# A graph attention layer on one core: longer DMA runs, four neighbouring nodes a partition, and Q in float32

## The chip, the cores and the metric

The kernel runs on one core of a Trainium2 chip. Five engines work side by side: TensorE (PE, with its weight loads shown apart as PEld), VectorE (DVE), ScalarE (ACT), GpSimd (POOL) and SyncE (SP), which issues most of the plain DMAs. The metric is the device time of one execution in microseconds; less is better. A profiled execution has a span, from its first to its last instruction, and a time that is a little longer.

## What is computed

The graph has 12500 nodes with 128 features and 212500 edges, sorted by destination. With 8 heads of 16 features:

```
Q, K, V = x @ WQ, x @ WK, x @ WV            # per node, then split into 8 heads
Eh      = edge_attr @ WE                    # per edge
score   = K[src] * Q[dst] / sqrt(16) * Eh
score   = exp(clip(score.sum(-1), -5, 5))   # one number per edge and head
wV, Z   = segment_sum(V[src] * score, dst), segment_sum(score, dst)
h       = x + wV / (Z + 1e-6)
y       = x + batchnorm(h) * gamma + beta   # statistics over all nodes
out     = layernorm(y)                      # per node
```

Everything is float32.

## The kernel before, in words

Edges come in tiles of 128, 1661 tiles in all. A *unit* is up to 4 tiles whose destinations lie in a window of 64 nodes; a *group* is two units, so 8 tiles, and there are NG = 208 groups. The two halves of a group sit on the upper and lower 64 partitions wherever nodes are on partitions.

**Table stage.** `table_rows` (L634) multiplies node features by WK and WV (L641: the features, `hx`, are the stationary operand, 128 columns of nodes at a time) and copies the products out with ACT and DVE in turn (L249, L250). Each call does four blocks of 128 nodes. A DMA on SP (L649) writes them to the table `kvd` in DRAM: node `c * 128 + p` comes from partition `p`, so one run is the 1 KB of one node. Meanwhile GpSimd gathers the source features of the first 8 groups straight from `x` (64 gathers); for these groups K and V are computed per edge (`project`, `project_main`).

**Gathers.** For all other groups GpSimd issues one indirect DMA per tile (L202): 128 rows of 1 KB from `kvd` into a slot. There are eight slots and one more that comes free later; a slot is free again when the `message` of its group is done (L580). `pace` and `issue` (L208 to L218) put the gathers in their places among the other engines' steps.

**Main loop** (L759). Iteration g runs, for several groups at once, the steps of a hand-written order. SP loads edge attributes for group g+4 (`load`, L433, three buffers of 4 KB a partition) and the *places*: for each edge of a unit, its destination's number inside the window. The places were turned by PE and written to `relT` in DRAM by `place` (L313); `load_rel` (L338) reads one group's, `load_quad` (L327) four groups' at once, spread over 64 partitions a half, four runs of 1 KB in each. On PE: `q_mm` (L483) makes Q of the window's nodes, `gather_sum` (L596, L595) adds the messages up by a one-hot matrix, `eh_mm` (L510) makes Eh, `turn_back` (L543) transposes, `qe_mm` (L525) spreads Q to the edges: the stationary operand is Q, the moving one a one-hot matrix of the places (`turned_onehot`, L473, bf16). Q is float32 and is split into three bf16 parts whose products are added: `q_out` (L487), `q_hi` (L491) and `q_mid` (L498) on ACT, `q_rest` (L495) and `q_lo` (L501) on DVE; so `qe_mm` has six matmuls a group, three for each half. On DVE further: `products` (L558), `scores` (L565), `both` (L535), `attn` (L612), `message` (L580), `onehot` (L463 to L466).

**Last stage** (L896). When the last group is added in, the batch norm's statistics are closed and 25 tiles of up to 512 nodes are centred, scaled and written. PE subtracts the mean over the features and turns nodes onto partitions in one matmul, with the nodes' features as the stationary operand: `part_of_x` (L740) and L941 for the nine tiles of `AHEAD`, L952 for the others, in which GpSimd or DVE first form the sum. Seven of the L740 tiles come before this stage begins. ACT squares (L967, L972), DVE scales (L984), and L986 writes 512 nodes with one DMA, 512 B a run. The last tile has 212 nodes. `load_x` (L414) brings the features back for this stage, in four DMAs of 512 columns a slot.

The lines of the changed functions and of their callers follow.

Of the kernel before, what the change touches and what calls it, by code (L numbers as in the profile page):

```python
# [21 lines left out]
G = 8  # L22
# [38 lines left out]
def gnn_kernel(  # L61
# [42 lines left out]
    kvd = dram.tile([N, 2 * P], F32, name="kvd")  # L104
    relT = dram.tile([T, P], BF16, name="relT")

# [81 lines left out]
    def slot(i):  # L188
        return rows.tile([P, 2 * G * P], F32, name=f"slot{i}")
# [123 lines left out]
    def place(r):  # L313
        nc.vector.tensor_copy(vw(rel, r), vw(rel_i, r))
        nc.vector.tensor_tensor(vw(rel, r), vw(rel, r), bc(base_f, r), op=OP.subtract)
        end = ustarts[r[0]] + (r[1] - r[0]) * r[2]
        for t in range(ustarts[r[0]], end, P):
            n = min(P, end - t)
            ps = spare_ps
            nc.tensor.transpose(ps[:n], rel[:, t:t + n], ident)  # L320
            row = wp.tile([P, P], BF16, name="relrow", bufs=2)
            nc.vector.tensor_copy(row[:n], ps[:n])  # L322
            nc.scalar.dma_start(relT[t:t + n, :], row[:n])

    RB = {}

    def load_quad(q):  # L327
        t = late[0].tile([P, RQ, U * P], BF16, name="rbq", bufs=2)
        for h in (0, 1):
            at = ustarts[2 * RQ * q + h] * P  # L330
            nc.sync.dma_start(t[h * WN:(h + 1) * WN], bass.AP(
                tensor=relT.tensor, offset=relT.offset + at, ap=[[0, WN], [G * P, RQ], [1, U * P]]))
        for k in range(RQ):
            RB[RQ * q + k] = t[:, k, :]

    quads = range(-(-2 * LATE // RQ), sizes.count(G) // RQ)

    def load_rel(g):  # L338
        if g // RQ in quads:
            return  # L340
        RB[g] = wp.tile([P, U * P], BF16, name="rb", bufs=3)
        for h in (0, 1):
            t, n = ustarts[2 * g + h], usizes[2 * g + h]
            nc.sync.dma_start(RB[g][h * WN:(h + 1) * WN, :n * P],
                              bass.AP(tensor=relT.tensor, offset=relT.offset + t * P, ap=[[0, WN], [1, n * P]]))

# [67 lines left out]
    def load_x():  # L414
        t = slot(free.pop(0))
        for k in range(4):
            if todo:
                i = todo.pop(0)
                XR[i] = t[:, k * B4:(k + 1) * B4]
                nc.sync.dma_start(XR[i][:, :width(i)], xT[:, i * B4:i * B4 + width(i)])  # L420

    EA, OH, OT, Q3, XW, BASE, MSG, QE, OS, AT, AGG, WT, PW = ({} for _ in range(13))

# [18 lines left out]
    def q_window(g):  # L442
        if g not in BASE:
            n = 2 if g % 2 == 0 and g + 1 < NG else 1
            _, at = nc.values_load_multi_w_load_instructions(
                base_i[0:1, 2 * g:2 * (g + n)], engines=(ET.Activation,), min_val=0, max_val=N,
                skip_runtime_bounds_check_because="node ids")
            for k in range(n):
                BASE[g + k] = at[2 * k:2 * k + 2]
        XW[g] = wp.tile([P, P], F32, name="xw", bufs=8)  # L450
        for h in (0, 1):
            nc.scalar.activation(XW[g][:, h * WN:(h + 1) * WN], hx[:, ds(BASE[g][h], WN)], AF.Copy)  # L452
# [16 lines left out]
    def turned_onehot(g):  # L469

        OT[g] = wp.tile([P, U * P], BF16, name="ot", bufs=2)
        if usizes[2 * g] == usizes[2 * g + 1] == U:
            nc.vector.tensor_scalar(OT[g], RB[g], wiota, None, op0=OP.is_equal)  # L473
# [5 lines left out]
    PQ, QS, QR = {}, {}, {}  # L479

# [4 lines left out]
    def q_out(g):  # L485
        QS[g] = wp.tile([P, P], F32, name="qs", bufs=2)
        nc.scalar.activation(QS[g], PQ[g], AF.Copy, scale=0.25)  # L487

    def q_hi(g):
        Q3[g] = wp.tile([P, 3, P], BF16, name="q3", bufs=2)  # L490
        nc.scalar.activation(Q3[g][:, 0, :], QS[g], AF.Copy)  # L491

    def q_rest(g):
        QR[g] = QS[g]
        nc.vector.tensor_sub(QR[g], QS[g], Q3[g][:, 0, :])  # L495

    def q_mid(g):
        nc.scalar.activation(Q3[g][:, 1, :], QR[g], AF.Copy)  # L498

    def q_lo(g):  # L500
        nc.vector.tensor_sub(Q3[g][:, 2, :], QR[g], Q3[g][:, 1, :])  # L501

# [17 lines left out]
    def qe_mm(g):  # L520
        QE[g] = [psp.tile([P, U * P], F32, name="ps_q", bufs=2)[:, :(b - a) * P] for a, b in halves(g)]
        for k in range(3):
            for h, (a, b) in enumerate(halves(g)):
                r = slice(h * WN, (h + 1) * WN)
                nc.tensor.matmul(QE[g][h], Q3[g][r, k, :], OT[g][r, :(b - a) * P], start=(k == 0), stop=(k == 2))  # L525

# [105 lines left out]
    NB = -(-N // P)  # L632

    def table_rows(b):  # L634
        t = table_tile(b // 4)
        for q in range(b, min(b + 4, NB), 2):
            ps = wide()
            m = min(2, NB - q)
            for i in range(m):
                n = min(P, N - (q + i) * P)  # L640
                nc.tensor.matmul(ps[:n, i, :], hx[:, (q + i) * P:(q + i) * P + n], w_kv, start=True, stop=True)  # L641
            fl = min(m, N // P - q)
# [4 lines left out]
        full = min(4, N // P - b)  # L647
        if full > 0:
            nc.sync.dma_start(kvd[b * P:(b + full) * P, :].rearrange("(c p) d -> p c d", p=P), t[:, :full, :])  # L649
# [11 lines left out]
    def both_halves(g):  # L661
# [3 lines left out]

    steps = [[(locate,)], [(place, runs[0])], [], [(q_mm, 0), (q_out, 0), (q_hi, 0)],
             [(q_rest, 0), (q_mid, 0), (load_rel, 0)], [(q_lo, 0), (load, 0)],
             [(q_mm, 1), (q_out, 1), (q_hi, 1), (load_rel, 1)],
             [(q_rest, 1), (q_mid, 1)], [(q_lo, 1), (load_rel, 2)], [(load, 1)], [(turned_onehot, 0)],
             [(turned_onehot, 1)]]  # L670
# [24 lines left out]
    table[0] = True  # L695
    load_kv()
    ehqe(0)
    q_mm(2)
    q_out(2)
    q_hi(2)  # L700
    both_halves(0)
    q_rest(2)
    q_mid(2)
    turn_back(0)
    ehqe(1)
    within(load, 2)
    turned_onehot(2)
    load_rel(3)
    q_window(3)
    q_window(4)  # L710
    q_mm(3)
    q_out(3)
    load_rel(4)
    load(3)
    onehot(0)
# [18 lines left out]
    def blocks(i):  # L734
        n = width(i)
        return [(k, min(P, n - k * P)) for k in range(-(-n // P))]

    def part_of_x(i, ps):
        for k, m in blocks(i):
            nc.tensor.matmul(ps[:m, k, :], XR[i][:, k * P:k * P + m], cent, start=(k == 0), stop=False)  # L740

# [17 lines left out]
    for g in range(NG - 2):  # L759
        within(load, g + 4)  # L760
        within(load_rel, g + 5)
        if (g + 6) % RQ == 0 and (g + 6) // RQ in quads:
            load_quad((g + 6) // RQ)
        within(q_hi, g + 3)
        within(products, g)
        within(q_lo, g + 2)
        within(denom, g - 2)
        within(scores, g)
        within(clip_exp, g)
        within(recip, g - 2)  # L770
        within(turned_onehot, g + 3)
        within(both_halves, g + 1)
# [4 lines left out]
        within(add_x, g - 3)  # L777
        within(q_mm, g + 4)
        if g < LATE + 4:
# [10 lines left out]
        within(x_out, g - 3)  # L790
        within(q_out, g + 4)
        within(sums_out, g - 1)
# [3 lines left out]
        within(eh_out, g + 2)  # L796
        within(q_window, g + 5)
        within(turn_back, g + 1)
        within(qe_mm, g + 2)
        within(attn, g - 2)  # L800
        within(q_rest, g + 3)
        within(q_mid, g + 3)
        within(message, g)
# [92 lines left out]
    def last_stage(fin, bank, PX):  # L896
# [35 lines left out]
        def centred(i):  # L932
# [16 lines left out]
            if not full:  # L949
                whole = i in on_vector  # L950
                for k, m in blocks(i):
                    nc.tensor.matmul(ps[:m, k, :], Y[i][:, k * P:k * P + m], cent, start=not whole,  # L952
                                     stop=(k == 3 or not whole))
# [22 lines left out]
        def scaled(p):  # L976
# [3 lines left out]
            for h, i in enumerate(p):  # L980
                bl = blocks(i)
                c, fb = i * B4, sum(m == P for _, m in bl)
                if fb:
                    nc.vector.tensor_tensor(o[:, h, :fb, :], PY[i][:, :fb, :],  # L984
                                            v[:, h, :fb, :].to_broadcast([P, fb, P]), op=OP.mult)
                    (nc.scalar if i == NY - 2 else nc.sync).dma_start(  # L986
                        out[c:c + fb * P, :].rearrange("(c p) d -> p c d", p=P), o[:, h, :fb, :])
                for k, m in bl[fb:]:
# [161 lines left out]
```

## Time and profile before

| | |
|---|---|
| median of 3 runs | 2141.86 us (2141.61 to 2143.22) |
| the profiled execution, its time | 2143.53 us |
| its span | 2141.1 us |
| mean granted PE clock | 0.917 of full speed |
| instructions | 31269 |
| DMA | 386.41 MB, mean 180 GB/s |
| DMA packets | 172648, 88727 of them under 2 KB |

In a row of groups stand the line, the engine, the operation, what it writes and reads, the shapes and the count; then the busy time in us and the mean of one in ns; then the idle time of the engine before them, and what ended it. In a row of the timeline stand the start and the duration in us, the engine, the line, the operation and, in brackets, the idle time before it. In a row of the windows stand the length, then the busy time and count of PE, PEld, DVE, ACT and POOL, the granted clock, the DMA engines' busy share and GB/s. In a row of DMA issues stand the count, the KB of each and the median us from issue to landing. PE's records of one float32 matmul are two, each with a weight load of its own.

### The profile page before, as it was taken

To read this page: it belongs to the slowest core of one execution; us is meant where nothing else is said; L and a number is where in the kernel's file an instruction comes from. 1 tells how busy PE (TensorE), PEld (TensorE's weight loads), DVE (VectorE), ACT (ScalarE), POOL (GpSimd) and SP (SyncE) were. 2 spreads that over 40 slices of the span, in tenths; PEclk is the share of its full clock that TensorE was granted. 3 is DMA by queue.
4 is the path that set the end of the run, shared out by engine and by line. 5 is a ranking of instruction groups with operands and counts; after the bars stand their busy time and mean duration, and the time that the engine had idled before them with its cause. 6 is when DMAs were issued, how large, how long until landed. Compare 5 with 4: busy or idle time off the path is not lost. (4 is left out here: it accounts for less than half of the span.)

```text
span 2141.1 us, 31269 instructions
## 1 busy us (share of the span) xinstructions
PE 1710.7 (80%) x9414; PEld 1100.9 (51%) x9414; DVE 1590.1 (74%) x3555; ACT 670.6 (31%) x2688; POOL 1606.6 (75%) x1697
## 2 busy tenths in 40 slices
PE   8899998777868778877778778777878877778777
PEld 7576565444545445544445445545545545544456
DVE  4679998777777777777677777677777777777786
ACT  3454343223223223222223223223223222223225
POOL 7777777777777777777777777777777777777775
PEclk9999999998998998899898998898898898898899
DMA  9957666565565565565565565565565565565574
GB/s 306 308 177 201 188 198 183 165 182 166 165 183 158 171 183 163 167 183 165 165 183 158 172 183 163 167 184 160 169 184 159 170 184 161 167 184 164 170 235 125
DMA packets 172648, 386.41 MB, mean 180 GB/s; under 512 B 35950, under 2 KB 88727, under 8 KB 172471
## 3 DMA queue, kind: packets, MB, share of 16 engines
q0 software_dynamic: 78704, 213.62, 34.6%
q1 hardware_dynamic: 90404, 169.36, 25.9%
q8 instruction: 78, 1.28, 0.3%
q10 hardware_dynamic: 3363, 1.34, 0.2%
q14 instruction: 99, 0.81, 0.1%
HBM read 364.56 MB, written 19.63 MB: 179 GB/s over the span
## 5 line engine op out<-in xcount | busy, mean ns | idle before, releaser
L202 POOL DMA_INDIRECT slot<-kvd,srcs x1597 | 1517.8, 950 | 486.4 <-issue 409.4
L558 DVE TENSOR_TENSOR slot<-slot,ps_t 128x512 f32<-128x512 f32 x410 | 276.7, 682 | 453.2 <-DMA slot<-kvd,srcs 412.3
L543 PE MATMUL ps_t<-ident,wt 128*128 128x128 f32 x1661 | 283.9, 313 | 385.9 <-DVE wt L535 384.1
L596 PE MATMUL ps_a<-msg,oh 128*128 128x136 f32 (+1 forms) x3322 | 524.4, 297 | 2.1 <-DVE msg L580 2.1
L543 PEld LDWEIGHTS ps_t<-ident,wt 128*128 128x128 f32 x1661 | 211.7, 159 | 562.3 <-issue 501.2
L596 PEld LDWEIGHTS ps_a<-msg,oh 128*128 128x128 f32 (+1 forms) x3322 | 425.2, 171 | 81.5 <-issue 53.8
L575 ACT ACTIVATE ps_m<-s 128x64 f32<-128x64 f32 (+1 forms) x209 | 47.5, 227 | 1125.4 <-DVE s L574 1060.9
L510 PE MATMUL ps_e<-ea,w_e 128*128 128x512 f32 x832 | 390.6, 591 | 0.7 <-ACT wt L517 0.7
L535 DVE TENSOR_TENSOR wt<-wt,ps_q 128x512 f32<-128x512 f32 x416 | 264.4, 675 | 2.6 <-PE ps_q L525 2.6
L580 DVE TENSOR_TENSOR msg<-slot,ps_m 128x1024 f32<-128x1024 f32 (+2 forms) x209 | 248.0, 1188 | 0.4 <-ACT ps_m L575 0.3
L565 DVE TENSOR_REDUCE s<-slot 128x64 f32<-128x1024 f32 (+1 forms) x208 | 248.1, 1194 | 0.1
L517 ACT ACTIVATE wt<-ps_e 128x512 f32<-128x512 f32 x416 | 233.8, 620 | 13.3 <-PE ps_e L510 13.2
L525 PE MATMUL ps_q<-ot,q 64*128 64x512 bf16 x1248 | 213.3, 457 | 0.0
L510 PEld LDWEIGHTS ps_e<-ea,w_e 128*128 128x128 f32 x832 | 143.0, 190 | 100.7 <-issue 98.5
L463 DVE TENSOR_TENSOR oh<-ps_m,rel_i 128x512 f32<-128x512 f32 x208 | 141.4, 680 | 0.0
L491 ACT ACTIVATE q<-qs 128x128 bf16<-128x128 f32 x208 | 64.3, 309 | 217.3 <-PE ps_q L525 186.6
L621 PEld LDWEIGHTS ps_a<-ident,at 128*128 128x128 f32 x408 | 71.7, 221 | 111.7 <-issue 56.0
L621 PE MATMUL ps_a<-ident,at 128*128 128x128 f32 x408 | 115.4, 370 | 2.5 <-DVE relrow L322 2.3
L626 ACT ACTIVATE hx<-ps_a 128x64 f32 x408 | 87.9, 215 | 33.9 <-PE ps_a L596 27.2
L452 ACT ACTIVATE xw<-hx 128x64 f32 x416 | 88.2, 280 | 11.1 <-DMA hx<-xT 6.5
L525 PEld LDWEIGHTS <-q 64*128 64x128 bf16 x1248 | 48.9, 103 | 80.9 <-issue 64.4
L622 PE MATMUL ps_a<-xw,ident 128*128 128x128 f32 x408 | 89.7, 306 | 0.0
(175 smaller groups left out, 1618.9 us busy)
## 6 DMA issues: line engine op xcount, KB each, us to landing
ea<-eaT SPq DMA_DIRECT2D x207, 512.0 KB, 3.8
slot<-kvd,srcs POOLq DMA_INDIRECT x1597
rbq<-relT SPq DMA_DIRECT2D x94, 256.0 KB, 6.6
kvd<-slot SPq DMA_DIRECT2D x12, 512.0 KB, 7.1
kvd<-t SPq DMA_DIRECT2D x12, 512.0 KB, 6.8
slot<-xT SPq DMA_DIRECT2D x24, 256.0 KB, 5.2
out<-o SPq DMA_DIRECT2D x23, 256.0 KB, 3.2
hx<-xT SPq DMA_DIRECT2D x11, 512.0 KB, 7.7
```

The lines of the kernel that those rows point to most:

```text
L202: return nc.gpsimd.indirect_dma_start(out=out, out_offset=None, in_=table, in_offset=bass.IndirectOffsetOnAxis(ap=srcs[:, e:e + 1], axis=0))
L463: nc.vector.tensor_tensor(one, iota_ps[:, None, :].to_broadcast([P, n, P]), r[:, :n, None].to_broadcast([P, n, P]), op=OP.is_equal)
L510: nc.tensor.matmul(eh, w_e, EA[g][:, a:b, :].rearrange("p a b -> p (a b)"), start=True, stop=True)
L517: nc.scalar.activation(t[:, :(b - a) * P], EH[g][h], AF.Copy)
L525: nc.tensor.matmul(QE[g][h], Q3[g][r, k, :], OT[g][r, :(b - a) * P], start=(k == 0), stop=(k == 2))
L535: nc.vector.tensor_tensor(t, t, QE[g][h], op=OP.mult)
L543: nc.tensor.transpose(ps[:, j, :], WT[g][h][:, j * P:(j + 1) * P], ident)
L558: step = nc.vector.tensor_tensor(kv, kv, PW[g][i][:, :b - a, :], op=OP.mult)
L565: step = nc.vector.tensor_reduce(SS[g][:, a:b, :], KV[g](a, b, 0).rearrange("p t (h d) -> p t h d", d=DH), axis=AX.X, op=OP.add)
L580: step = nc.vector.tensor_tensor(MSG[g][:, a:b, :P].rearrange("p t (h d) -> p t h d", d=DH), KV[g](a, b, P).rearrange("p t (h d) -> p t h ...
L596: nc.tensor.matmul(AGG[g][WN if j >= n else 0:], OH[g][j], MSG[g][:, j, :], start=(j == 0), stop=(j == n - 1))
L621: nc.tensor.matmul(ps, AT[g], ident, start=True, stop=False)
```

## The change

- `load` fetches the attributes of two groups in one DMA: 8 KB a run for 4 KB, two buffers of two groups for three of one.
- `place` orders the turned places so that all first units stand together in `relT` and all second units after them (a DVE copy ahead of the transpose, and two DMAs for one); the places past the last full group go to a second tensor, `rel_end`. Four groups' places of a half are then one run of 4 KB for four of 1 KB.
- `table_rows` takes every fourth column of 512 nodes as the stationary operand, so that a partition holds four neighbouring nodes and the write to `kvd` has runs of 4 KB for 1 KB. The last stage does the same in L740, L941 and L952, and its writes have runs of 2 KB for 512 B. Tiles that aren't full stay as they were.
- `load_x` fetches a slot's features in one DMA.
- Q stays in one float32 tile, the turned one-hot is float32 too, and `qe_mm` has two matmuls a group. `q_hi`, `q_rest`, `q_mid` and `q_lo` are gone.
- Some steps run for a group one or two later in the order: `load_rel` g+3 for g+5, `q_mm` and `q_out` g+2 for g+4, `turned_onehot` g+2 for g+3, `q_window` g+3 for g+5; buffers of `rb` 2 for 3, `xw` 6 for 8, `qs` 1 for 2.

```diff
     def load_quad(q):
         for h in (0, 1):
-            at = ustarts[2 * RQ * q + h] * P
-            nc.sync.dma_start(t[h * WN:(h + 1) * WN], bass.AP(
-                tensor=relT.tensor, offset=relT.offset + at, ap=[[0, WN], [G * P, RQ], [1, U * P]]))
+            nc.sync.dma_start(t[h * WN:(h + 1) * WN].rearrange("p a b -> p (a b)"), places(h, RQ * q, RQ))
...
-    def load(g):
-        n = nt(g)
-        EA[g] = wp.tile([P, G, P], F32, name="ea", bufs=3)
-        nc.sync.dma_start(EA[g][:, :n, :].rearrange("p a b -> p (a b)"),
-                          eaT[:, starts[g] * P:(starts[g] + n) * P])
+    def load(i):
+        gs = range(2 * i, min(2 * i + 2, NG))
...
+        t, n = wp.tile([P, 2, G, P], F32, name="ea", bufs=2), sum(nt(g) for g in gs)
...
+        nc.sync.dma_start(t.rearrange("p c a b -> p (c a b)")[:, :n * P],
+                          eaT[:, starts[2 * i] * P:(starts[2 * i] + n) * P])
...
-        OT[g] = wp.tile([P, U * P], BF16, name="ot", bufs=2)
+        OT[g] = wp.tile([P, U * P], F32, name="ot", bufs=2)
...
-        for k in range(3):
-            for h, (a, b) in enumerate(halves(g)):
-                r = slice(h * WN, (h + 1) * WN)
-                nc.tensor.matmul(QE[g][h], Q3[g][r, k, :], OT[g][r, :(b - a) * P], start=(k == 0), stop=(k == 2))
+        for h, (a, b) in enumerate(halves(g)):
+            r = slice(h * WN, (h + 1) * WN)
+            nc.tensor.matmul(QE[g][h], QS[g][r], OT[g][r, :(b - a) * P], start=True, stop=True)
...
+    def every_fourth(a, k):
+        return a.rearrange("p (n c) -> p n c", c=4)[:, :, k]
...
-                nc.tensor.matmul(ps[:n, i, :], hx[:, (q + i) * P:(q + i) * P + n], w_kv, start=True, stop=True)
+                at = every_fourth(hx[:, b * P:(b + 4) * P], q + i - b) if b + 4 <= N // P else \
+                    hx[:, (q + i) * P:(q + i) * P + n]
+                nc.tensor.matmul(ps[:n, i, :], at, w_kv, start=True, stop=True)
...
+            nc.sync.dma_start(kvd[b * P:(b + 4) * P, :].rearrange("(p c) d -> p c d", c=4), t)
...
+    def nodes(a, i, k, m):
+        return every_fourth(a[:, :B4], k) if width(i) == B4 else a[:, k * P:k * P + m]
...
-            nc.tensor.matmul(ps[:m, k, :], XR[i][:, k * P:k * P + m], cent, start=(k == 0), stop=False)
+            nc.tensor.matmul(ps[:m, k, :], nodes(XR[i], i, k, m), cent, start=(k == 0), stop=False)
...
-        within(load, g + 4)
-        within(load_rel, g + 5)
+        if g % 2 == 0:
+            load(g // 2 + 2)
+        within(load_rel, g + 3)
...
-        within(q_hi, g + 3)
         within(products, g)
-        within(q_lo, g + 2)
...
-        within(turned_onehot, g + 3)
+        within(turned_onehot, g + 2)
...
-        within(q_mm, g + 4)
+        within(q_mm, g + 2)
...
-                    nc.tensor.matmul(ps[:m, k, :], hx[:, c + k * P:c + k * P + m], scaled_cent, start=False,
+                    nc.tensor.matmul(ps[:m, k, :], nodes(hx[:, c:c + width(i)], i, k, m), scaled_cent, start=False,
                                      stop=False)
...
-                    nc.tensor.matmul(ps[:m, k, :], Y[i][:, k * P:k * P + m], cent, start=not whole,
+                    nc.tensor.matmul(ps[:m, k, :], nodes(Y[i], i, k, m), cent, start=not whole,
```

More of the change, by code (lines that the diff above doesn't have):

```diff
@@ L663, in both_halves @@
         both(g, 1)
[L666 to L669, printed above, removed]
+    steps = [[(locate,)], [(place, runs[0])], [], [(q_mm, 0), (q_out, 0)],
+             [(load_rel, 0)], [(load, 0)], [(load_rel, 1)], [], [], [], [(turned_onehot, 0)],
              [(turned_onehot, 1)]]
@@ L696, in gnn_kernel @@
     load_kv()
+    load(1)
+    load_rel(2)
     ehqe(0)
-    q_mm(2)
-    q_out(2)
-    q_hi(2)
+    q_mm(1)
+    q_out(1)
     both_halves(0)
-    q_rest(2)
-    q_mid(2)
     turn_back(0)
     ehqe(1)
[L706 to L714, printed above, removed]
     onehot(0)
@@ L790, in gnn_kernel @@
         within(x_out, g - 3)
-        within(q_out, g + 4)
+        within(q_out, g + 2)
         within(sums_out, g - 1)
@@ L796, in gnn_kernel @@
         within(eh_out, g + 2)
-        within(q_window, g + 5)
+        within(q_window, g + 3)
         within(turn_back, g + 1)
```

75 lines of the change are left out of this document (43 added, 32 removed).

## The prediction

> **What bounds the kernel now.** I read the engine totals first, then the groups of GpSimd (POOL), then its timeline at both ends.
>
> ```profile
> PE 1710.7 (80%) x9414; PEld 1100.9 (51%) x9414; DVE 1590.1 (74%) x3555; ACT 670.6 (31%) x2688; POOL 1606.6 (75%) x1697
> ...
> L202 POOL DMA_INDIRECT slot<-kvd,srcs x1597 | 1517.8, 950 | 486.4 <-issue 409.4
> ```
> ```profile
> L202 POOL DMA_INDIRECT slot<-x,srcs x64 | 60.8, 951 | 21.1 <-issue 14.6 <-DMA slot<-x,srcs 2.7 <-DMA srcs<-src 1.9
> ```
> ```profile
> 3.04 1.15 POOL L202 DMA_INDIRECT slot<-x,srcs  x1 [1.87 <-DMA srcs<-src]
> ...
> 2085.13 0.95 POOL L202 DMA_INDIRECT slot<-kvd,srcs  x1 [0.30 <-issue]
> 2086.38 0.95 POOL L202 DMA_INDIRECT slot<-kvd,srcs  x1 [0.30 <-issue]
> ```
>
> By busy shares PE looks like the bound; it isn't. The 1597 gathers take 950 ns each with 486.4 / 1597 = 0.305 us before each, and the last rows show 0.30 as the plain step from one gather to the next. From 3.04 to 2087.33 us there are 1661 gathers, 1.255 us apiece on average, back to back: none waits for a slot, for the table or for a semaphore long enough to show. So the time is three parts: 3.0 us until the first gather, 2084.3 us of gathers, 53.8 us after the last one. An edit counts only where it (a) shortens or lengthens a gather, (b) makes GpSimd wait, or (c) touches the last 53.8 us. Almost all of this change, the DMA runs above all, is none of these.
>
> The last part has a bound of its own:
>
> ```profile
> 2100.00:2127.80 27.80, 27.74 (x225) 25.85 (x223) 24.20 (x46) 23.41 (x105) 25.98 (x26) 1.00 0.57 163
> ```
> ```profile
> 2096.56 1.95 PE L740 MATMUL ps_t<-cent,slot 128*128 128x128 f32 x16
> 2098.35 1.06 PE L740 MATMUL ps_a<-cent,slot 128*128 128x128 f32 x8
> ...
> 2112.02 1.95 PE L952 MATMUL ps_q<-cent,y 128*128 128x128 f32 x16
> 2113.81 1.06 PE L740 MATMUL ps_t<-cent,slot 128*128 128x128 f32 x8
> ```
>
> The first row is the window view (PE busy, weight loads, DVE, ACT, POOL, clock, DMA share): PE is busy 27.74 of 27.80 us, at full clock. The timeline under it gives its pace: the 16 matmul records from 2112.02, each with its own weight load, take 2113.81 - 2112.02 = 1.79 us, 0.112 us a record. Here PE has no slack.
>
> **The change part by part.**
>
> *Gathers and the DVE operations beside them.* The diff removes `q_rest` and `q_lo` (L495, L501), two DVE operations a group with both inputs in SBUF.
>
> ```profile
> L501 DVE TENSOR_TENSOR q<-qs,q 128x128 bf16<-128x128 f32 x208 | 59.7, 287 | 0.0
> L495 DVE TENSOR_TENSOR qs<-qs,q 128x128 f32<-128x128 f32 x208 | 58.5, 281 | 0.0
> ```
> ```profile
> 99.63 0.28 DVE L495 TENSOR_TENSOR qs<-qs,q 128x128 f32<-128x128 f32 x1
> 99.65 1.08 POOL L202 DMA_INDIRECT slot<-kvd,srcs  x1 [0.30 <-issue]
> ...
> 2031.24 0.28 DVE L495 TENSOR_TENSOR qs<-qs,q 128x128 f32<-128x128 f32 x1
> 2031.30 1.03 POOL L202 DMA_INDIRECT slot<-kvd,srcs  x1 [0.30 <-DVE wt L535]
> ```
>
> A gather that starts while L495 runs is long: 1.08 and 1.03 us against 0.94 to 0.95. These are the first and the last of 49 such gathers in the timeline, 4.9 us over the usual length together; L501 has 5 more, 0.4 us. Both operations go, so I take -5. Ends: 0, if another operation moves into the same place, and 1661 x (0.950 - 0.940) = -17, if every excess went; I keep 0 to -10, as other operations remain. [...]
>
> *Weight loads of every fourth column.* `every_fourth` makes the stationary operand of the table's matmuls (L641) and of the last stage's (L740, L941, L952) 128 columns 16 bytes apart instead of side by side. No row of before loads weights like that. The nearest:
>
> ```profile
> L596 PEld LDWEIGHTS ps_a<-msg,oh 128*64 128x64 f32 x1660 | 187.1, 138 | 29.0 <-issue 3.9
> ...
> L525 PEld LDWEIGHTS <-q 64*128 64x128 bf16 x1248 | 48.9, 103 | 80.9 <-issue 64.4
> ...
> L595 PEld LDWEIGHTS ps_a<-os,carry 64*1 64x1 f32 x414 | 16.9, 77 | 38.9 <-issue 38.9
> ...
> L952 PEld LDWEIGHTS ps_q<-cent,y 128*128 128x128 f32 x24 | 2.9, 192 | 0.0
> ```
>
> 1, 64 and 128 float32 columns take 77, 138 and 192 ns: (192 - 77) / 127 = 0.91 ns a column, 116 ns for 128. That is the 0.112 us from record to record above, so a load is as long as the matmul that hides it, and anything added to it shows. 128 bf16 columns take 103 ns: the float32 load is limited by reading, not by filling the array. Ends: if it goes by elements it stays 0.112; if by the stretch that it covers (512 columns), it is four times that, 0.448 us. I take double, 0.224, the middle in ratio. Nearness to a row doesn't decide between ends, but a load at its reading limit makes "free" the less likely one. [...]
>
> In the last stage that is 24 full tiles x 8 records (nine L941, fifteen L952), and the five L740 tiles that stand after 2096.5 us (4, 5, 6, 12, 18), 40 more: 232 records x 0.112 = +26.0 us. ACT and GpSimd, at 23.41 and 25.98 of 27.80, fall behind PE and add nothing. Before 2096.5 the L740 of tiles 2 and 3 stand in front of critical matmuls, each 8 x 0.112 = 0.9 us longer: at most +1.8. At the end ACT is no longer a pair of tiles behind PE, which gives about as much back. I put the two together at zero, within 2 us.
>
> In the table stage a matmul is 256 columns:
>
> ```profile
> 17.34 1.03 PE L641 MATMUL ps_e<-w_kv,hx 128*128 128x256 f32 x4
> 18.21 1.03 PE L641 MATMUL ps_q<-w_kv,hx 128*128 128x256 f32 x4
> ...
> 75.56 0.90 SPq L652 DMA_DIRECT2D kvd<-slot  x1
> ...
> 82.14 0.94 POOL L202 DMA_INDIRECT slot<-x,srcs  x1 [0.30 <-DVE q L501]
> 83.39 0.95 POOL L202 DMA_INDIRECT slot<-kvd,srcs  x1 [0.30 <-issue]
> ```
> ```profile
> kvd<-slot SPq DMA_DIRECT2D x1, 128.0 KB, 3.9
> ```
>
> 4 records in 0.87 us, 0.217 each: a doubled load of 0.224 costs 24 x 8 x 0.007 = 1.3 us. The table's last write is issued by 76.46; with the 3.9 us of its neighbour it lands near 80.4, and the first gather from it starts at 83.39 without a wait: 3 us of cover. So 0 at double, but at four times 192 x 0.231 = 44 us, of which 41 stop GpSimd.
>
> *Longer runs.* They speed the DMA engines, which GpSimd doesn't wait for. The table's writes may land earlier, but the gathers from x run until 83.1 anyway. The result's last two writes (the 212-node tile) keep their form. 0, at most -1.
>
> *Q in float32.*
>
> ```profile
> L510 PE MATMUL ps_e<-ea,w_e 128*128 128x512 f32 x832 | 390.6, 591 | 0.7 <-ACT wt L517 0.7
> ...
> L525 PE MATMUL ps_q<-ot,q 64*128 64x512 bf16 x1248 | 213.3, 457 | 0.0
> ```
> ```profile
> L463 DVE TENSOR_TENSOR oh<-ps_m,rel_i 128x512 f32<-128x512 f32 x208 | 141.4, 680 | 0.0
> ...
> L473 DVE TENSOR_SCALAR ot<-rbq,wiota 128x512 bf16<-128x512 bf16 x188 | 62.1, 330 | 0.2 <-issue 0.2
> ```
> ```profile
> 1000.00:1200.00 200.00, 152.90 (x824) 95.32 (x824) 148.04 (x334) 57.47 (x240) 151.28 (x160) 0.90 0.57 167
> ```
>
> Six bf16 matmuls a group take 213.3 / 208 = 1.03 us; two float32 ones like L510 take 390.6 / 416 = 0.94 each, 0.94 if the two row halves still run together, 1.88 if not. So PE gets -0.1 to +0.85 us on 7.7 of 10.0 us a group: hidden behind the gathers. The turned one-hot in float32 costs DVE up to 0.35 us (680 ns, as L463 takes for 512 float32 columns, less 330), less than the 0.57 that L495 and L501 free. `q_out` now feeds `qe_mm` in its own iteration; between them on PE stand `gather_sum`, `eh_mm` and `turn_back`, so the wait is covered. The program's own order shows GpSimd's gathers in the same sequence as before.
>
> *Fewer buffers* (attributes, places, windows). The loads come one iteration later than before, still one ahead of their use. The cover is thinnest at the start, where the compute lags:
>
> ```profile
> ea<-eaT SPq DMA_DIRECT2D x207, 512.0 KB, 3.8
> ```
> ```profile
> 160.00:180.00 20.00, 20.00 (x127) 13.19 (x126) 19.82 (x45) 9.30 (x36) 15.32 (x16) 1.00 0.78 215
> ```
> ```profile
> 162.03 1.21 DVE L580 TENSOR_TENSOR msg<-slot,ps_m 128x1024 f32<-128x1024 f32 x1
> ...
> 173.92 0.94 POOL L202 DMA_INDIRECT slot<-kvd,srcs  x1 [0.30 <-issue]
> ```
>
> The message of group 8 ends at 163.24 and frees the slot that the gathers of group 17 fill from 173.92: 10.7 us of slack, the least of all groups. Eight groups x 0.85 us of PE is 6.8, so no gather waits unless 4 us come on top.
>
> Sum: +26 (last stage) - 5 (gathers) = +21. Against the profiled execution, 2143.53 us with a span of 2141.1, that is 2164.5; against the median of 2141.86 it is **2162.9**. The profiled run stands 1.7 above that median, so I work from the median.
>
> **The rivals.**
>
> 1. *Spread loads are free, and the port waits go* (the other side: faster). Place: the 54 long gathers. Price: -5.3, so 2136.6. It decides wherever the last stage's record stays at 0.112 us; each 0.01 us more costs 2.3 us, so from 0.135 the sign turns. For it: the loads' time per column may go by elements alone. Against: the load has no reserve in reading. [...]
> 2. *Loads free, waits stay*: L612, also two SBUF inputs, or L473 moves into the gathers' start as DVE runs 0.2 us earlier. About 2141.5.
> 3. *Loads four times as long*: 232 x 0.336 = +78 at the end, +41 at the table, -5: 2256. Against: nothing in the rows; it is the end of the bound.
> 4. *The start stops GpSimd*: 6.8 us of PE, and the first two double loads, 3.8 us longer each, waited for in full: 14.4 - 10.7 = 3.7 us. With free loads 2140.3, with doubled ones 2166.6. Against: that needs every bound at its worst end.
>
> **How the numbers follow.** Forecast 0.53 (own range 2150 to 2173: a record of 0.16 to 0.25 us, gathers 0 to -10); rival 1 0.25, rival 2 0.09, rival 3 0.10, rival 4 0.03. A measurement of this kernel can tell about 0.2%, 4.3 us. Faster by more (under 2137.6): 0.25; within: 0.09; slower (over 2146.1): 0.66. The range must take in rival 1 with its bound and may leave out rival 3 and the ends: 2133 to 2173.
>
> **What would show it.** Right: weight loads of L740, L941 and L952 (their new lines) near 300 ns in the last stage, 8 records in 1.8 us, the stretch after the last gather near 80 us. Wrong: 192 ns and 0.9 us there. For the gathers: last one ending near 2082, fewer than 30 over 0.99 us; if it ends at 2087 or later, the port waits moved. An idle time over 0.31 before any gather shows rival 3 or 4, at 83 us or near 170 us.

## The result and the profile after

The changed kernel takes **2172.73 us** (median of 4 runs, 2172.01 to 2178.01), the kernel before 2142.18 beside it (2141.61 to 2143.22): ratio **1.0147**, 95% interval 1.013 to 1.0165. Beside another run of the kernel before, the changed one gave 2171.76 against 2142.8, ratio 1.0134 (1.0117 to 1.0151). The forecast was 2162.9: slower, as it came, but 9.8 us too little.

On some of the chips that the experiments ran on, the kernel before takes 2741 to 2769 us instead of 2142; a total from such a chip is only set against the total of the kernel before on the same chip. In the traces from there GpSimd often waits for slots: it is idle for 1056 to 1103 us before its gathers in all, for 508 to 510 on the other chips.

The profiled execution took 2172.01 us, its span is 2170.1 us, 29.0 more than before. First the page's engine totals and GpSimd's group of gathers:

```profile
PE 1786.2 (82%) x8998; PEld 1151.6 (53%) x8998; DVE 1540.6 (71%) x3152; ACT 578.1 (27%) x2272; POOL 1607.7 (74%) x1697
...
L205 POOL DMA_INDIRECT slot<-kvd,srcs x1597 | 1519.0, 951 | 488.8 <-issue 417.2
```

PE has 416 matmul records fewer and is busy 75 us longer; `qe_mm` alone (now L529) takes 288.5 us instead of 213.3. The gathers are busy 1519.0 - 1517.8 = 1.2 us longer and idle 488.8 - 486.4 = 2.4 us longer. The timeline of GpSimd shows where the idle time is, and the end of the last gather:

```profile
82.24 0.95 POOL L205 DMA_INDIRECT slot<-x,srcs  x1 [0.30 <-issue]
85.58 0.94 POOL L205 DMA_INDIRECT slot<-kvd,srcs  x1 [2.40 <-DMA kvd<-slot]
...
2089.97 0.94 POOL L205 DMA_INDIRECT slot<-kvd,srcs  x1 [0.30 <-DVE s L578]
```

The first gather from the table waits for the table's write, 2.40 us instead of the usual 0.30. The last ends at 2090.91, 3.6 us later than before (2087.33); after it come 2170.1 - 2090.91 = 79.2 us instead of 53.8, so **25.4 of the 29.0 us are in the last stage**. There the window view, the timeline of PE and the groups of weight loads answer to the rows of before:

```profile
2100.00:2127.80 27.80, 27.80 (x127) 26.89 (x126) 13.62 (x31) 10.73 (x43) 14.12 (x16) 1.00 0.11 39
```
```profile
2150.24 1.92 PE L951 MATMUL ps_q<-cent,y 128*128 128x128 f32 x8
2151.99 3.90 PE L951 MATMUL ps_t<-cent,y 128*128 128x128 f32 x16
2155.72 2.03 PE L951 MATMUL ps_a<-cent,y 128*128 128x128 f32 x8
```
```profile
L940 PEld LDWEIGHTS ps_t<-scaled_cent,hx 128*128 128x128 f32 x24 | 5.9, 328 | 0.0
L742 PEld LDWEIGHTS ps_t<-cent,slot 128*128 128x128 f32 x24 | 5.8, 329 | 0.0
L951 PEld LDWEIGHTS ps_t<-cent,y 128*128 128x128 f32 x24 | 5.8, 329 | 0.0
```

PE is busy for all of the 27.80 us and does 127 matmul records where it did 225. A load takes 328 to 329 ns instead of 192, and 16 records take 2155.72 - 2151.99 = 3.73 us, 0.233 each instead of 0.112. DVE, ACT and GpSimd fell from 23 to 26 us to 11 to 14: they now wait for PE.

### The profile page after: what moved, and what is told of

It reads as the page before. It is cut to its first block, busy times and chain, and to the rows that moved or that the text cites. A ratio compares the mean times of both kernels' runs of the same rounds, so it can differ in the third digit from the quotient of the medians.

```text
span 2170.1 us, 29265 instructions
## 1 busy us (share of the span) xinstructions
PE 1786.2 (82%) x8998; PEld 1151.6 (53%) x8998; DVE 1540.6 (71%) x3152; ACT 578.1 (27%) x2272; POOL 1607.7 (74%) x1697
## 3 DMA queue, kind: packets, MB, share of 16 engines
q1 hardware_dynamic: 36740, 169.36, 22.7%
## 5 line engine op out<-in xcount | busy, mean ns | idle before, releaser
L205 POOL DMA_INDIRECT slot<-kvd,srcs x1597 | 1519.0, 951 | 488.8 <-issue 417.2
L547 PE MATMUL ps_t<-ident,wt 128*128 128x128 f32 x1661 | 276.7, 313 | 345.4 <-DVE wt L539 344.6
L600 PE MATMUL ps_a<-msg,oh 128*128 128x136 f32 (+1 forms) x3322 | 515.8, 293 | 0.0
L600 PEld LDWEIGHTS ps_a<-msg,oh 128*128 128x128 f32 (+1 forms) x3322 | 417.2, 168 | 77.6 <-issue 50.6
L529 PE MATMUL ps_q<-ot,qs 64*128 64x512 f32 x832 | 288.5, 776 | 0.0
L625 PE MATMUL ps_a<-ident,at 128*128 128x128 f32 x408 | 110.5, 357 | 2.5 <-DVE relrow L332 2.3
L630 ACT ACTIVATE hx<-ps_a 128x64 f32 x408 | 88.6, 217 | 86.4 <-PE ps_a L600 77.6
L529 PEld LDWEIGHTS ps_q<-ot,qs 64*128 64x128 f32 x832 | 74.1, 218 | 45.0 <-ACT wt L522 23.7
L485 DVE TENSOR_TENSOR oh<-ps_m,rel_i 128x256 f32<-128x256 f32 x208 | 86.7, 417 | 0.0
L502 PE MATMUL ps_a<-w_q,xw 128*128 128x128 f32 x416 | 86.3, 292 | 0.0
```

The source lines that it names most:

```text
L205: return nc.gpsimd.indirect_dma_start(out=out, out_offset=None, in_=table, in_offset=bass.IndirectOffsetOnAxis(ap=srcs[:, e:e + 1], axis=0))
L529: nc.tensor.matmul(QE[g][h], QS[g][r], OT[g][r, :(b - a) * P], start=True, stop=True)
L547: nc.tensor.transpose(ps[:, j, :], WT[g][h][:, j * P:(j + 1) * P], ident)
L600: nc.tensor.matmul(AGG[g][WN if j >= n else 0:], OH[g][j], MSG[g][:, j, :], start=(j == 0), stop=(j == n - 1))
L625: nc.tensor.matmul(ps, AT[g], ident, start=True, stop=False)
```

## The experiments

A weight load of 128 neighbouring columns is called near below, one of every fourth column spread. *Port waits*, in the expectations, are what gathers that start beside DVE operations take over the usual 0.943 us.

**1. The last stage's loads near again, the writes as changed.**

```diff
-        return every_fourth(a[:, :B4], k) if width(i) == B4 else a[:, k * P:k * P + m]
+        return a[:, k * P:k * P + m]
```

> The changed kernel, with the stationary operands of the last stage (L742, L940, L951) back to 128 neighbouring columns; the result is still written with four neighbouring nodes a partition, so its rows come in another order inside each block of 512, which no time depends on. Theory (spread weight loads set the pace of a saturated PE): loads back at 190 to 192 ns, 8 records in about 0.9 us, the stretch after the last gather 53 to 55 us instead of 79.2, the total 2172.7 - 25 = 2147 to 2149 (what is left over the kernel before is the stop at the table and the port waits, 3.4 us). Rival (the writes by four nodes a partition, or Q in float32 with fewer buffers, make the end late): the stretch stays near 79 us and the total near 2172.

2757.06 us where the kernel before takes 2743.25, ratio 1.0051 (1.0028 to 1.0074). Its last gather, by the timeline of GpSimd:

```profile
2638.40 0.95 POOL L205 DMA_INDIRECT slot<-kvd,srcs  x1 [1.16 <-DVE rz L609]
```

The span is 2744.5, so 105.2 us come after it. All stretches on these chips are longer: messages still follow for 57 to 62 us after the last gather, on the others for 5 to 10. What counts is the comparison with the next three kernels.

**2. The kernel before with the last stage alone changed** (`nodes` and the writes of the changed kernel).

> The kernel before with only the last stage changed: every fourth column as the stationary operand and the result written by four neighbouring nodes a partition. Theory: loads at 325 to 330 ns, the stretch after the last gather 53.8 + 25.4 = 79 us, gathers unchanged to 2087.3, total 2142 + 25.4 = 2167.5. Rival (the rest of the change makes the end late): near 2142.

2774.04 us, ratio 1.0105 (1.0056 to 1.0155).

```profile
2643.68 0.94 POOL L202 DMA_INDIRECT slot<-kvd,srcs  x1 [1.92 <-issue]
```

Span 2780.2: 135.6 us after the last gather, 30.4 more than in experiment 1, at loads of 320 to 330 ns.

**3. The table's loads near, and all loads and writes near.**

```diff
-                at = every_fourth(hx[:, b * P:(b + 4) * P], q + i - b) if b + 4 <= N // P else \
-                    hx[:, (q + i) * P:(q + i) * P + n]
+                at = hx[:, (q + i) * P:(q + i) * P + n]
```

> The changed kernel, with only the stationary operands of the table (L650) back to 128 neighbouring columns, the table still written with four rows a partition (its rows in another order inside each block of 512). Theory (the slower table loads make the table 5 us late and GpSimd waits 2.1 us over the usual step for it): no gather waits more than 0.31 us near 83 us, the last gather ends 2 to 2.5 us earlier, at 2088.4 to 2089, total near 2170.4, the last stage unchanged at 79 us. Rival (the table is late for its writes, or for something else in the first 60 us): the wait of 2.4 us stays, total 2172.5.

> The changed kernel with both loads near and both writes in their old form: what stays of the change are the longer runs for attributes, places and x, Q in float32 and the buffers. Theory: the kernel before plus the moved port waits, 1.1 us: last gather near 2088.5, after it 53.8 us, total 2141.5 to 2144.5. Rival (Q in float32 or the buffers cost by themselves): above 2146. Forecast of the record (port waits go, 5 us): 2137.

table_near: 2782.25, ratio 1.013 (1.0083 to 1.0176), 133.1 us after the last gather; once more (table_near_2) on another such chip 2779.37, 1.0111 (1.0079 to 1.0144), 132.5 us. near_all: 2763.38, 1.0062 (1.004 to 1.0084), 105.4 us; once more (near_all_2) 2759.96, 1.0051 (1.0034 to 1.0068), 105.6 us. So the stretch goes by the last stage's loads: 105 us with near ones, 132 to 136 with spread ones, whatever the table, the runs and Q do. Counted from the end of the last message, the last stage is even the same on both kinds of chips. These are the last messages of before, near_all, after and before_far_tail:

```profile
2092.04 0.89 DVE L580 TENSOR_TENSOR msg<-slot,ps_m 128x384 f32<-128x384 f32 x2 [0.25 <-ACT ps_m L575]
2717.73 0.89 DVE L584 TENSOR_TENSOR msg<-slot,ps_m 128x384 f32<-128x384 f32 x2 [0.25 <-ACT ps_m L579]
2096.81 0.89 DVE L584 TENSOR_TENSOR msg<-slot,ps_m 128x384 f32<-128x384 f32 x2 [1.48 <-ACT ps_m L579]
2705.36 0.88 DVE L580 TENSOR_TENSOR msg<-slot,ps_m 128x384 f32<-128x384 f32 x2 [1.49 <-ACT ps_m L575]
```

After them come 48.2 and 46.6 us with near loads, 72.4 and 74.0 with spread ones. All other runs but that of experiment 4 have 46 to 48 or 72 to 73. tail_near, which differs from the changed kernel in these loads alone, has 46.3: the spread loads cost 26.1 us of the last stage.

The rest of the change is not free on these chips: near_all takes 18 to 20 us more than the kernel before. Its last gather ends at 2659.76, that of before_far_tail, which is the kernel before up to the last stage, at 2644.62; which part of the change does it stays open (experiment 8).

What was asked of the table was not to be seen: on these chips GpSimd waits 4.8 to 8 us there in every kernel.

**4. Other steps between the columns**, three in one kernel.

```diff
-            nc.tensor.matmul(ps[:m, k, :], nodes(XR[i], i, k, m), cent, start=(k == 0), stop=False)
+            nc.tensor.matmul(ps[:m, k, :], nodes(XR[i], i, k, m, 2), cent, start=(k == 0), stop=False)
...
+        return a[:, :P * s].rearrange("p (n s) -> p n s", s=s)[:, :, k % s]
```

> The changed kernel with other steps between the 128 columns of the last stage's stationary operands: every second in part_of_x (L742), every third for the sums (L951 in the changed kernel), every eighth for hx (L940); the nodes that are multiplied are partly the wrong ones, the number and size of the matmuls are the same. Known: step 1 takes 190 to 192 ns, step 4 takes 325 to 330. Theory A (reading goes by 16-byte lines, two hits a line hide it): step 2 near 192, step 3 between, step 8 near 330. Theory B (by the stretch covered): step 2 near 238, step 3 near 284, step 8 near 510. Theory C (any step other than 1 costs the same): all near 330.

The groups of weight loads, step 8 first, then 3, then 2:

```profile
L942 PEld LDWEIGHTS ps_t<-scaled_cent,hx 128*128 128x128 f32 x24 | 5.9, 332 | 0.0
L953 PEld LDWEIGHTS ps_m<-cent,y 128*128 128x128 f32 x24 | 4.5, 261 | 0.1
L744 PEld LDWEIGHTS ps_t<-cent,slot 128*128 128x128 f32 x24 | 3.0, 197 | 0.0
```

192, 197, 261, 329 and 332 ns for steps 1, 2, 3, 4 and 8: the times of theory A. Counted in stretches of 16 bytes, called lines here, the 128 columns lie on 32, 64, 96, 128 and 128. Over the 77 ns of one column, 128 lines cost 252 ns, 1.97 a line, and 96 cost 184, 1.92 a line; 64 lines cost 120, just over the 115 that 128 neighbouring columns take anyway. All five fit a load that takes 77 ns and, on top, the longer of 0.9 ns a column and about 1.95 ns a line; over the 77 ns, step 4 takes 2.2 times what step 1 does. This is a fit to five times: the runs show what a load costs by its step, not how the memory is read.

**5. Two neighbouring nodes a partition in place of four**, beside the changed kernel and the kernel before on a chip where the latter takes 2142.8.

```diff
+    def every_other(a, k):
+        return a[:, k // 2 * 2 * P:(k // 2 + 1) * 2 * P].rearrange("p (n c) -> p n c", c=2)[:, :, k % 2]
```

> The changed kernel with two neighbouring nodes a partition in place of four: every second column as the stationary operand in the table and in the last stage, runs of 2 KB to the table and of 1 KB to the result. Theory (reading goes by 16-byte lines, two columns a line hide it; only the loads make the end late): loads at 196 to 198 ns in place of 325 to 330, 8 records of the last stage in 0.90 to 0.95 us, so 25 us less than the changed kernel on the same chip. Rival (any step between columns costs the last stage its pace, or the writes by neighbouring nodes do): within 5 us of the changed kernel.

> The changed kernel itself, beside the kernel before on the same chip. Where the kernel before takes 2142: 2172.7, ratio 1.0147. Where it takes 2742 (as beside the kernels run so far): the last stage's 25 us and the 12 to 20 us that near_all cost there, 2780 to 2790, ratio 1.014 to 1.017.

> The kernel before, for its trace on the chip of this call. If the gathers follow one another without a wait, the last ends near 2087 and the time is 2142. If the time is near 2742: PE, ACT and DVE stop together every 25 to 40 us, as they do in near_all, and GpSimd waits 540 to 590 us for slots in all; stops shorter than near_all's, since Q is made four groups ahead and PE need not wait for it.

pairs: **2143.91** us, ratio 1.0006 (0.9996 to 1.0015); the changed kernel 2171.76; the kernel before 2141.25 in its one run, its gathers end at 2085.27. In pairs:

```profile
L952 PEld LDWEIGHTS ps_e<-cent,y 128*128 128x128 f32 x34 | 4.5, 196 | 0.1
```
```profile
2113.66 2.05 PE L952 MATMUL ps_q<-cent,y 128*128 128x128 f32 x16
2115.55 1.11 PE L743 MATMUL ps_t<-cent,slot 128*128 128x128 f32 x8
```
```profile
84.19 0.94 POOL L205 DMA_INDIRECT slot<-kvd,srcs  x1 [1.01 <-issue]
...
2088.14 0.95 POOL L205 DMA_INDIRECT slot<-kvd,srcs  x1 [0.30 <-DVE at L616]
```

A record takes 1.89 / 16 = 0.118 us, and 2141.4 - 2089.08 = 52.3 us come after the last gather, against 82.3 in the changed kernel and 53.5 in the kernel before of this chip. Two nodes in place of four take the 28 us away and keep runs of 1 and 2 KB. But nothing is gained over the kernel before: the longer runs, Q in float32 and the buffers together are worth 0 on this chip (-0.04% to +0.15%).

**6. The first attribute DMA later.** In the changed kernel the table's last write is issued at 81.19 us, 75.56 before; its spread loads explain 192 x (0.233 - 0.217) = 3.1 us of the 5.6. The queue of SP shows an attribute DMA just ahead of a piece of the features (before, then after):

```profile
46.83 0.50 SPq L433 DMA_DIRECT2D ea<-eaT  x1
47.37 0.85 SPq L133 DMA_DIRECT2D hx<-xT  x1
```
```profile
49.84 0.43 SPq L452 DMA_DIRECT2D ea<-eaT  x1
50.31 0.84 SPq L136 DMA_DIRECT2D hx<-xT  x1
```

and ACT's timeline a wait before the next window copy (before, then after); while ACT waits, it copies no part of the table out, and PE stands, 4.43 us ahead of L275 (3.22 before, ahead of L272):

```profile
55.76 0.40 ACT L452 ACTIVATE xw<-hx 128x64 f32 x2 [4.41 <-DMA rb<-relT]
```
```profile
60.83 0.40 ACT L471 ACTIVATE xw<-hx 128x64 f32 x2 [7.52 <-DMA hx<-xT]
```

The row of before names the places, but there too the piece of the features lands just ahead of the copy, at 55.69 us by the trace; after, it lands at 60.73.

late_attributes moves `load` four steps later; no_turned leaves out `turned_onehot` for all groups but two; late_no_turned does both:

```diff
-             [(load_rel, 0)], [(load, 0)], [(load_rel, 1)], [], [], [], [(turned_onehot, 0)],
+             [(load_rel, 0)], [], [(load_rel, 1)], [], [], [], [(load, 0)], [(turned_onehot, 0)],
...
+        if g > 1:
+            OT[g] = OT[g % 2]
+            return
```

> The changed kernel with one step moved: the first attribute DMA (1 MB) is issued four steps later in the table stage, behind three more pieces of the features and writes. Theory (ahead of the piece of the features that ACT's first window copy waits for, it holds up ACT, so the table's copies, so PE): ACT's wait before L471 near 58 us falls from 7 to 4 or 5 us, the table's last write is issued 2 to 3 us earlier than the changed kernel's 81.2 to 81.9, GpSimd's stop of 2.1 to 2.4 us before the first gather from the table falls under 0.7, total 1.5 to 2.5 us under the changed kernel, 2169.5 to 2171. Rival (the loads with every fourth column alone make the table late): the stop stays at 2.1 to 2.4 us.

> The changed kernel without turned_onehot from the third group on: its DVE operation (L492, 0.47 us a group) is left out and the first two groups' one-hot matrices are used for all, so the scores are other numbers. Theory (waits move, since the eight gathers of a group and the DVE operations of a group keep one rhythm): the sum over 0.943 us stays at 9 to 13 us. Rival (an operation's waits go with it): it falls by what stands beside L492, 5 to 7 us, to 5 to 8, and the last gather ends at 2084 to 2086 instead of 2089.5 to 2090.9.

> The changed kernel with the first attribute DMA four steps later and without turned_onehot from the third group on (the first two groups' one-hot matrices are used for all). Two readings of one trace, on a chip where the kernel before takes 2142. Gather near 83 us: by the theory (the DMA held up ACT's window copy) it waits under 0.7 us in place of 2.4 to 2.75, by the rival (the loads alone) still over 2. Sum of the gathers over 0.943 us: by the theory that waits move, 9 to 13 us as before; by the rival that an operation's waits go with it, 5 to 8. Total 2167 to 2170 if stop and waits go, 2169.5 to 2171 if the stop alone goes.

> The same kernel as late_no_turned. On a chip where the kernel before takes 2142: gather near 83 us, under 0.7 us of wait by the theory, over 2 by the rival. Sum of the gathers over 0.943 us: after the 17 to 21 us that attn's operation brought on the other chips once turned_onehot was gone, 10 to 20 us here by the theory that waits move; 5 to 8 by the rival.

late_attributes (2802.9, ratio 1.0109, 1.0083 to 1.0136), no_turned (2789.47), late_no_turned (2791.43) and late_no_turned_2, the same kernel again (2785.0), fell on chips where the kernel before takes 2742 to 2769: the wait at the table says nothing there. late_no_turned_3, the same once more, fell on one where it takes 2144.42: **2165.59** us in its one run, span 2163.4. The moved DMA, in the queue of SP, ACT and GpSimd:

```profile
48.95 0.43 SPq L136 DMA_DIRECT2D hx<-xT  x1
...
58.45 1.88 SPq L452 DMA_DIRECT2D ea<-eaT  x1
```
```profile
55.23 0.40 ACT L471 ACTIVATE xw<-hx 128x64 f32 x2 [2.33 <-DMA hx<-xT]
```
```profile
83.60 0.95 POOL L205 DMA_INDIRECT slot<-kvd,srcs  x1 [0.30 <-issue]
...
2081.78 0.95 POOL L205 DMA_INDIRECT slot<-kvd,srcs  x1 [0.30 <-issue]
```

The stop is gone, at spread loads, and the table's last write is issued at 76.41. From the issue of that piece of the features to ACT's copy it took 6.3 us with no attribute DMA ahead of it (48.95 to 55.23), 8.4 with 512 KB (47.37 to 55.76) and 10.5 with 1 MB (50.31 to 60.83): 2.1 us for each 512 KB, from one trace each. Pairs, with 1 MB ahead too, has 10.1 (48.37 to 58.44).

**7. The gathers' waits.** Summed over the timeline of GpSimd, the gathers took this much over 0.943 us: 12.3 and 10.3 us in the two traces of before, 13.4 and 11.9 in those of after, 12.9 in pairs. Beside which DVE operation a long gather starts tells what it waited for. Before: 44 end with L495 (4.5 us), 12 with the turned one-hot (1.1), 11 with `attn` (0.9). After: 36 with the turned one-hot (4.7 us), 38 with `attn` (2.5), 17 with the sum of the scores (1.3). Two of the 36, and the one-hot's groups before and after:

```profile
125.55 0.43 DVE L492 TENSOR_SCALAR ot<-rb,wiota 128x512 f32<-128x512 bf16 x1
125.71 1.09 POOL L205 DMA_INDIRECT slot<-kvd,srcs  x1 [0.30 <-PE ps_a L625]
...
1971.76 0.43 DVE L492 TENSOR_SCALAR ot<-rbq,wiota 128x512 f32<-128x512 bf16 x1
1971.83 1.18 POOL L205 DMA_INDIRECT slot<-kvd,srcs  x1 [0.30 <-issue]
```
```profile
L473 DVE TENSOR_SCALAR ot<-rbq,wiota 128x512 bf16<-128x512 bf16 x188 | 62.1, 330 | 0.2 <-issue 0.2
```
```profile
L492 DVE TENSOR_SCALAR ot<-rbq,wiota 128x512 f32<-128x512 bf16 x188 | 84.8, 451 | 0.0
```

A gather that starts while the operation runs waits for its end: 1.09 and 1.18 us in place of 0.94. In the trace of after, 35 gathers start more than 0.04 us after the one-hot and over 0.15 us before its end: each takes longer by the time that was left less 0.13 us, to within 0.01. The gathers that start up to 0.3 us ahead of it take at most 0.03 us longer. So a longer operation keeps a gather longer, and catches more of them: had the one-hot ended 0.12 us sooner, as the bf16 one did (330 ns for 451), these 35 would have waited 1.3 us in all instead of 4.7, by an estimate from their starts. The second pair of traces (before_2, after_2) agrees: L495 and `q_lo` gave 3.0 us there, the one-hot rose from 1.9 to 4.5, `attn` from 0.3 to 1.9.

L495 and `attn` read two tensors in SBUF, the one-hot reads one and a number a partition: gathers are held up beside all three (1.08 us in before, 1.06 in no_turned, 1.18 in after), so two tensors as inputs are not the condition. What it is that holds a gather no run shows. Without the turned one-hot, the group of gathers is this in late_no_turned_3 and in late_no_turned (on a chip where GpSimd waits for slots):

```profile
L205 POOL DMA_INDIRECT slot<-kvd,srcs x1597 | 1512.9, 947 | 486.6 <-issue 432.9 <-DMA slot<-kvd,srcs 11.0 <-DVE wt L541 8.8
```
```profile
L205 POOL DMA_INDIRECT slot<-kvd,srcs x1597 | 1526.0, 956 | 1034.6 <-DVE rz L611 476.2 <-issue 433.6 <-DVE msg L586 58.4
```

In the first, 1519.0 - 1512.9 = 6.1 us less than after, with the last gather's end at 2082.73: the waits went with the operation (7.5 us over 0.943 in all), and the theory that they always move was wrong there. In the second they grew, to 20.7 us in sum (16.9 in no_turned, 18.3 in late_no_turned_2), where the changed kernel's variants with the one-hot have 6 to 10 on such chips: `attn` now holds up 113 gathers. The first and the last such pair in no_turned, 117 in all:

```profile
324.95 0.35 DVE L618 SCALAR_TENSOR_TENSOR at<-os,keep,rz 128x128 f32<-128x128 f32 x1
325.05 1.06 POOL L205 DMA_INDIRECT slot<-kvd,srcs  x1 [0.30 <-issue]
...
2646.74 0.35 DVE L618 SCALAR_TENSOR_TENSOR at<-os,keep,rz 128x128 f32<-128x128 f32 x1
2646.85 1.06 POOL L205 DMA_INDIRECT slot<-kvd,srcs  x1 [0.30 <-issue]
```

So an operation's waits go with it; what comes in their place hangs on where the next operations then stand against the gathers.

**8. Q in float32 alone, and the better parts together.**

```diff
-        Q3[g] = wp.tile([P, 3, P], BF16, name="q3", bufs=2)
...
+                nc.tensor.matmul(QE[g][h], QS[g][r], OT[g][r, :(b - a) * P], start=True, stop=True)
```

> The kernel before with Q in float32 alone: q_hi, q_rest, q_mid, q_lo gone, qe_mm with two matmuls a group, the turned one-hot in float32; all loads, buffers and the order as before (qs has three buffers). Theory (the port waits move to other DVE operations): the 54 long gathers beside q_rest and q_lo go, and as many come beside others; excess over the usual gather 11 to 14 us as before and as in the changed kernel, total 2141 to 2144. Rival (the record's: they go): excess 5 to 8 us, total 2136 to 2138.

> Two neighbouring nodes a partition (as in pairs) and the first attribute DMA four steps later. Theory: no gather waits over 0.35 us, 0.7 us less than pairs: 2142 to 2144 where the kernel before takes 2142.8, so no difference that can be told from it. Rival (the moved DMA makes the first group late instead): an idle time over 1 us before a gather, 2145 or more.

q32_alone: 2753.47 against 2741.47, ratio 1.0032 (1.0012 to 1.0051), and again (q32_alone_2) on another chip 2758.74 against 2769.37, 0.9967 (0.9947 to 0.9987). The two contradict each other, so these chips tell nothing of it; on a chip where the kernel before takes 2142 it did not run. pairs_late: 2775.75 against 2769.37, 1.002 (0.9999 to 1.0042): not told from the kernel before. No version here is shown to beat it.

## Why the prediction was wrong, and where it was right

- **What bounds it: right.** On a chip like the first profile's the time is the start, the gathers and the last stage, and nothing else of the change shows.
- **Weight loads of the last stage: right, in mechanism and size.** Forecast +26.0 at a record of 0.224 us; it came to 0.233, 232 x 0.121 = 28.1, and 25.4 in the profiled pair (28.8 in the second pair). That the size fits was luck: double was chosen between one and four times for no more than being in the middle. What the runs show of the size is experiment 4: the time fits the number of 16-byte lines. By the whole stretch covered, the bound that gave rival 3, step 8 would cost about twice step 4; it takes 332 ns for 329. That a load of neighbouring columns is limited by reading, without reserve, was inferred from 103 against 192 ns alone, and no run shows it; on twice the lines (step 2) a load takes 197.
- **"Both operations go, so I take -5": the step that failed most.** They went, with 5.0 us of waits. But the same edit made the turned one-hot float32; the up to 0.35 us that this adds (it came to 0.12) were counted as DVE time only, not as time in which a gather is held up. Its waits rose from 1.1 to 4.7 us, those of `attn` from 0.9 to 2.5. Sum +1.1 in place of -5: 6 of the 9.8 us missing. Rival 2 had L473 (now L492) and `attn` as what would hold up the gathers in their place, but by moving; for the one-hot it was mostly its length (experiment 7). What the prediction had named as the sign came: the last gather ended after 2087, and 75 gathers took over 0.99 us. With the one-hot left out for all groups but two (late_no_turned_3) the sum is 7.5: 4.8 less than before. That a port is behind these waits, as the prediction's name for them has it, no run shows; the runs show that a gather that starts while L495, the one-hot or `attn` runs takes longer (up to 1.08, 1.18 and 1.06 us in the rows shown, for 0.94).
- **The table, "0 at double", and "longer runs ... 0, at most -1": failed, 2.4 us.** The loads' part was 3.1 us, not 1.3, since the record came to 0.233. By the cover of 3 us that alone would have shown little: pairs, whose last write is late by 78.86 - 75.56 = 3.3 us, though its table records take the 0.217 us of before, has 0.7 us of stop. The rest is a longer run that does harm: the first attribute DMA has twice the bytes and stands ahead of a piece that ACT needs. The text said of the runs that they speed the DMA engines and that GpSimd doesn't wait for these. They do speed them: the packets of the queue `q1` take 25.9% of the 16 engines' span before and 22.7% after, for 169.36 MB in both, in 90404 packets and in 36740. It left out that ACT waits for them (7.52 us in place of 4.41), and PE for ACT, and the table for PE.
- **Q in float32 on PE, fewer buffers: right on such a chip.** `qe_mm` takes 288.5 / 208 = 1.39 us a group instead of 1.03, within the -0.1 to +0.85 forecast, and no gather after the first from the table waits over 0.5 us. On the chips of near_all the same part is not free.
- **The rest.** 8.6 us are these two steps and -0.6 the last stage; the remaining 1.8 is that the profiled run of before stood 1.7 above its median, and that of after 0.7 below its own, 2.4 together; 0.5 of it goes off again, since the time exceeds the span by 2.4 us before and by 1.9 after. The prediction's own range, 2150 to 2173, doesn't follow from the ends it names: a record of 0.16 with the gathers at -10 gives 2143, one of 0.25 with 0 gives 2174.
- **Rival 1 (faster) fell** with the record of 0.233 us. Rival 3's sign, an idle time at 83 us, did appear, though the loads were not four times as long; rival 4's, one near 170 us, did not. That a longer DMA stops the table by way of ACT was in no rival.

## What to carry to other kernels

Before strided weight loads go on a busy TensorE, count the 16-byte lines of the stationary operand: here two float32 columns a line cost almost nothing (0.118 us a record for 0.112) and one doubled the record (0.233). Where longer runs to DRAM are wanted, two neighbours a partition bring half the run of four and here almost none of its price (52.3 us after the last gather for 82.3, and 53.5 before); no longer run of this case gained time. When an operation that holds up gathers is removed, look at what the same edit makes longer on the same engine (here the one-hot, 451 ns for 330, with waits of 4.7 us for 1.1). And a DMA that was made longer held up here the piece behind it in its queue, by 2.1 us for each 512 KB: look for the engine that waits for such a piece.

## What the hardware showed that was not expected

- A bf16 load of neighbouring columns (`pick`, L946) has 210 ns beside loads with step 4, 106 in pairs, 100 before. That a load's record takes in time of the load beside it would fit this; no run tests it.
- On chips where the kernel before takes 2741 to 2769 us, DVE, ACT and PE stop together. In near_all's second run DVE's operation ahead of each group waits so 66 times, by the view of its line:

```profile
L482 DVE TENSOR_TENSOR oh<-ps_m,rel_i x208: 552/691/694, 107.8 to 2716.5; 128x512 f32<-128x512 f32 x104
its engine sat idle before it (us, times) until:
  remote: 648.9, 66
```

The view names no engine and no DMA as what ended these waits (`remote`); the same view of the changed kernel's second run shows no such wait. One of the 66 in near_all's first run lasts 11.35 us for DVE, to 1045.68 us, 14.05 for ACT's L630, and 12.75 for PE, which then waits for ACT. Around it the windows have PE without a record from 1034 to 1046 us, at a granted clock of 0.64 in the first half and 0.50 in the second, after 0.89 from 1010 to 1034. The mean granted clock is 0.818 in near_all's second run and 0.917 in the profiled run of before. That the clock is the cause is not shown; the cause stays open.
